# A graph network's gated step: one PSUM bank per graph in the last layer's gates

## The chip, the core and the metric

The kernel runs on one core of a Trainium2 chip. The core has a matrix engine (TensorE, PE in the profile), VectorE (DVE), ScalarE (ACT), GpSimd (POOL) and a queue engine for transfers (SyncE, SP). Matrix products are written to PSUM, eight banks of 512 f32 values for each of 128 partitions; PE writes them, ScalarE and VectorE read them. The metric is the time of one execution on the device, in microseconds (us); the median of three runs is given.

## The reference, cut to what matters

128 graphs of 128 nodes with 256 features each, and a 0/1 adjacency matrix per graph. First a normalisation and three layers of a gated network, then an attention layer. One gated layer is:

```
m    = h @ weight[i]
aggr = einsum('bst,bsd->btd', A, m)
gi   = aggr @ w_ih.T + b_ih          # split into i_r, i_z, i_n
gh   = h @ w_hh.T + b_hh             # split into h_r, h_z, h_n
r    = sigmoid(i_r + h_r)
z    = sigmoid(i_z + h_z)
n    = tanh(i_n + r * h_n)
h    = (1 - z) * n + z * h
```

Per graph the r and z gates thus need one sum over two products (state and edges), while n needs the two products apart: four blocks of columns, h_n, r, z, i_n.

## The kernel before, in words

The graphs are taken in 32 groups of 4. A group goes through three layers, called steps or turns here; the steps of three groups are interleaved by the list `turns`, so there are 96 gated steps in all. Steps of layers 0 and 1 (`gru`) compute the gates with features on partitions; the last layer's step (`gru_rows`) computes them with nodes on partitions, so that its result lies as the attention needs it.

The 2 x 2 blocks of each weight product are done in seven products in place of eight, with sums of blocks prepared ahead (`block_sums` for weights, `node_sums` for data). `products` writes the seven in order and adds them up in three pairs of PSUM banks, x, y and q. Each pair is one bank "rz" and one bank "n", each a tile of its own: x_rz, x_n, y_rz, y_n, q_rz, q_n. Two more banks, misc, serve the rest. The order is: product 1 into x, copied to y; product 5 (7 in the last step) into q; product 6 into y, copied to t2 in SBUF; the next into y, copied to t3, to which q is added by VectorE; then product 2 into x, one more into y, one more into q, which is added to t2. After that x, y, t2 and t3 each hold the sums for one quarter of the outputs; ScalarE takes the tanh of r and z from them, VectorE combines them with n.

In steps of layers 0 and 1 the data moves and the weights stand in the array: bank rz holds r and z for two graphs (256 columns each), bank n the two parts of n. In the last step the data stands in the array and the weights move: bank rz holds, for each of two graphs, r and z (a product of 256 columns), bank n for each graph h_n and i_n (products of 128 columns). There x and q are filled beforehand with the biases ("seeds", `seed`, from seed_x and seed_q). An f32 product stands as two records in the profile.

All work is recorded as operations with an engine, an assumed duration and the buffers (or parts of them) that they read and write. `Plan.run` orders them with these assumed durations, by due times; products of the gates keep their order as a chain. Then the operations are issued in that order, each engine working through its own list. Semaphores are not written by hand: the framework below derives them from the order and from which tiles each instruction reads and writes. Tiles are made by `make` from the table `BUFS`.

Names and lines of the profile: products of layers 0 and 1 are line 694, of the last step line 701; copies out of PSUM `put`, line 733 (737 and 739 for n with a bias); VectorE's addition of q, line 743; seeds, line 726; tanh of the gates, lines 789 and 807 (last step 837); edge sums, line 621; attention's products, lines 650 and 1077.

Of the kernel before, what the change touches and what calls it, by code (L numbers as in the profile page):

```python
# [16 lines left out]
P = 128  # L17
# [198 lines left out]
def kernel(  # L216
# [67 lines left out]
        "w1_sum": (1, "all", const, [P, D]),  # L284
    }
    DTYPE = {"at": I32, "a": BF16, "pl": U16, "plT": U16, "pe": U16, "peT": U16, "p3": BF16}
    phys = {}

    def make(tag, n, kind, pool, shape):
        for s in range(SETS if kind == "set" else 1):  # L290
            for k in range(n):
                phys[tag, s, k] = pool.tile(shape, DTYPE.get(tag, F32), name=f"{tag}_{s}{k}")
# [47 lines left out]
    def nat(b):  # L340
        return plain(b)[:, :3 * KD * D].rearrange("p (c e) -> p c e", e=D)

    def turned(src, dst, evict):

        for a in range(2):
            for k in range(KD):
                ps = bank()

                def turn(k=k, a=a, ps=ps):
                    for c in range(3):  # L350
                        nc.tensor.transpose(flat(ps)[:, c * P:(c + 1) * P],
                                            nat(src)[:, 3 * a + c, k * P:(k + 1) * P], ident)
                op("PE", 330, turn, [(src, a, a + 1)], [ps])
                to_sbuf(evict[k % len(evict)], 3 * P, ps, dst[k], 3 * P * a)

# [24 lines left out]
    def weights():  # L380
# [47 lines left out]
        homes = [[buf("h1"), last("hT")] for _ in range(L)]  # L428
        for layer in range(L):
            if layer == 1:  # L430
                turned(w_hh_nat, w_hhT, ("DVE", "ACT"))
                block_sums(w_hhT, W["s_hh"], "POOL", 1000)
            wT, half, msg = uT[layer // 2], layer % 2, w_msg[layer]
            for e in range(KD):
                ps = bank(layer == 0)

                def turn(ps=ps, e=e, msg=msg):
                    for k in range(KD):
                        nc.tensor.transpose(flat(ps)[:, k * P:(k + 1) * P],
                                            square(msg)[:, k, e * P:(e + 1) * P], ident)  # L440
                op("PE", 220, turn, [msg], [ps])
                to_sbuf("ACT", D, ps, wT, half * GN + e * D)
            w_x = homes[layer]
            for k in range(KD):
                for g0, gn in ((0, 512), (512, 3 * D - 512)):
                    ps = bank(layer == 0)

                    def compose(k=k, g0=g0, gn=gn, ps=ps, wT=wT, half=half):
                        for e in range(KD):
                            nc.tensor.matmul(  # L450
                                flat(ps)[:, :gn],
                                ap(wT)[:, half, e * D + k * P:e * D + (k + 1) * P],
                                plain(w_ihT[e])[:, g0:g0 + gn], start=(e == 0), stop=(e == KD - 1))
                    op("PE", 4 * gn * 27 // 32, compose,
                       [(wT, half * GN, (half + 1) * GN)] + w_ihT, [ps])
                    to_sbuf("DVE", gn, ps, w_x[k], g0)
            block_sums(w_x, W[f"s_x{layer}"], *(("POOL", 1000) if layer else ("DVE", 560)))
            if layer == 0:
                load_msg(2, [W["s_x0"]])
# [13 lines left out]

        def seeds():
            nc.gpsimd.tensor_tensor(plain(tmp[0]), plain(tmp[0]), plain(tmp[1]), OP.add)
            for t, q in ((tmp[0], 0), (tmp[2], 2)):
                nc.gpsimd.tensor_copy(ap(W["seed_x"])[:, q:q + 2, :], halves(t, 0))
                nc.gpsimd.tensor_tensor(ap(W["seed_q"])[:, q:q + 2, :], halves(t, 1), halves(t, 0),
                                        OP.subtract)
        op("POOL", 4000, seeds, tmp, [W["seed_x"], W["seed_q"]] + tmp[:1])  # L480

# [190 lines left out]
    DATA = [None, 0, 2, 3, 7, 4, 6, 5]  # L672
    R, Z, NN = 0, 1, 2

    def product(bank, i, parts, first, rows=False):


        def unit(t, w):
            return (t, DATA[i], DATA[i] + 1) if DATA[i] < 4 else (w, DATA[i] - 4, DATA[i] - 3)

        def source(t, w):
            if DATA[i] < 4:
                return ap(t)[:, DATA[i] // 2, (DATA[i] % 2) * H:(DATA[i] % 2 + 1) * H]
            return ap(w)[:, DATA[i] - 4, :]

        todo = []
        for term in range(max(len(p) for _, p in parts)):
# [3 lines left out]
        for c, chunk in enumerate(todo):  # L691
            def mm(c=c, chunk=chunk):
                for m, (half, q, w, t, sums) in enumerate(chunk):
                    nc.tensor.matmul(ap(bank)[:, half, :], ap(w)[:, i - 1, q, :], source(t, sums),  # L694
                                     start=(first and c == 0 and m == 0), stop=False,
                                     skip_group_check=True)

            def mm_rows(chunk=chunk):
                half, q, w, t, sums = chunk[0]
                for m in range(2):  # L700
                    nc.tensor.matmul(  # L701
                        ap(bank)[:, m, half * P:(half + len(chunk)) * P],
                        source(t, sums)[:, m * N:(m + 1) * N],
                        ap(w)[:, i - 1, q:q + len(chunk), :].rearrange("p q m -> p (q m)"),
                        start=False, stop=False, skip_group_check=True)
            plan.cursor += 432 * len(chunk) * SLOT // GATES
            op("PE", 432 * len(chunk), mm_rows if rows else mm,
               [unit(t, s) for _, _, _, t, s in chunk] + [(w, i - 1, i) for _, _, w, _, _ in chunk],
               [bank], due=plan.cursor)

    def products(layer, hT, hs, aT, gs, rows=False):

# [6 lines left out]
        state, edges = (W["s_hh"], hT, hs), (W[f"s_x{layer}"], aT, gs)  # L719
        kinds = (("rz", ((R, (state, edges)), (Z, (state, edges)))),  # L720
                 ("n", ((NN, (state,)), (NN, (edges,)))))
        X, Y, Q, T2, T3 = ({} for _ in range(5))

        def seed(b, kind, t):
            q = 0 if kind == "rz" else 2
            op("ACT", 590, lambda: nc.scalar.copy(
                ap(b), ap(t)[:, q:q + 2].rearrange("p (o q) m -> p o (q m)", o=1)
                .to_broadcast([P, 2, 2 * P])), [t], [b])

        def put(t, y, bias=None, mark=None):  # L730

# [13 lines left out]
        for kind, parts in kinds:  # L745
            X[kind], Y[kind] = buf("x_" + kind), buf("y_" + kind)
            if rows:
                seed(X[kind], kind, W["seed_x"])
            product(X[kind], 1, parts, not rows, rows=rows)
            put(Y[kind], X[kind], 1 if kind == "n" else None, mark=(plan.group, layer, kind))  # L750
        for kind, parts in kinds:
            Q[kind] = buf("q_" + kind)
            if rows:
                seed(Q[kind], kind, W["seed_q"])
            product(Q[kind], five, parts, not rows, rows=rows)
        for kind, parts in kinds:
            product(Y[kind], 6, parts, False, rows=rows)
            T2[kind] = buf("t2_" + kind)
            put(T2[kind], Y[kind], 2 if kind == "n" else None)
        for kind, parts in kinds:  # L760
            product(Y[kind], seven, parts, False, rows=rows)
            T3[kind] = buf("t3_" + kind)
            put(T3[kind], Y[kind])
            add(T3[kind], Q[kind])
        for kind, parts in kinds:
            product(X[kind], 2, parts, False, rows=rows)
        for kind, parts in kinds:
            product(Y[kind], four, parts, False, rows=rows)
        for kind, parts in kinds:
            product(Q[kind], three, parts, False, rows=rows)  # L770
            add(T2[kind], Q[kind])

        y, t2 = ((0, 1), (1, 0)) if rows else ((1, 0), (0, 1))
# [52 lines left out]
    def gru_rows(layer, hT, hs, aT, gs, rows, x1):  # L826
# [6 lines left out]
        for j, n, src in blocks:  # L833
            i = 2 * n + j
            outs, graphs = slice(j * P, (j + 1) * P), slice(2 * n, 2 * n + 2)
            s_rz, nn = src["rz"], src["n"]
            op("ACT", 700, lambda outs=outs, graphs=graphs, s_rz=s_rz: nc.scalar.activation(
                ap(rz).rearrange("p q (g d) -> p g q d", g=G)[:, graphs, :, outs],
                ap(s_rz).rearrange("p g (q m) -> p g q m", q=2), AF.Tanh, scale=0.5),
               [s_rz], [(rz, i, i + 1), (rz, 4 + i, 5 + i)])  # L840
            op("DVE", 422, lambda outs=outs, graphs=graphs, nn=nn: nc.vector.scalar_tensor_tensor(
                view(u)[:, graphs, outs],
                ap(rz)[:, 0].rearrange("p (g d) -> p g d", g=G)[:, graphs, outs], 1.0,
                ap(nn)[:, :, 0:P], op0=OP.add, op1=OP.mult),
               [nn, (rz, i, i + 1)], [(u, i, i + 1)], two=nn.tag[0] == "t")
            op("DVE", 422, lambda outs=outs, graphs=graphs, nn=nn: nc.vector.scalar_tensor_tensor(
                view(u)[:, graphs, outs], view(u)[:, graphs, outs], 0.5, ap(nn)[:, :, P:2 * P],
                op0=OP.mult, op1=OP.add),
               [nn], [(u, i, i + 1)], two=nn.tag[0] == "t")
        for n in (1, 0):  # L850
            d, lo, hi = buf("d"), 2 * n, 2 * n + 2
            cols = slice(n * GN, (n + 1) * GN)
# [340 lines left out]
```

## Time and profile before

| what | us |
|---|---|
| median of three runs | 2104.47 (2102.91 to 2105.32) |
| the profiled execution's own time | 2102.59 |
| its span, first to last instruction | 2100.6 |
| TensorE busy | 2086.8 (99%) |
| TensorE weight loads | 1862.0 (89%) |
| VectorE busy | 1668.5 (79%) |
| ScalarE busy | 1592.4 (76%) |
| GpSimd busy | 938.0 (45%) |

Records of matrix products overlap: a record lasts longer than the distance to the next one's start, so what a product costs is read from start to start in the timeline. A line of the timeline gives start, duration, engine, line, operation, tiles (out<-in), shape and number of merged records; in brackets stands the engine's idle time before it and who ended it. A line of the waits gives who waited for whom, the total in us, the number of times and the longest.

### The profile page before, as it was taken

Reading aid. Unit: us, or ns where it says so; the run is one execution under the profiler, and the core shown is the slowest. Engines: PE = TensorE matmul, PEld = TensorE weight load, DVE = VectorE, ACT = ScalarE, POOL = GpSimd, SP = SyncE. Lnnn points to the kernel's source line nnn. Section 1 sums busy time; section 2 is a strip of 40 time slices with the busy share of each in tenths; the row PEclk is TensorE's granted clock in tenths of the full one; section 3 lists DMA queues with packets and bytes.
Section 4 is the critical chain, followed back from the end, with each engine's and each line's share of the span. In section 5 each row is a group of like instructions: output and inputs, shape, how many; then the busy total and the mean of one; then the engine's idle time right before and its main releaser. Section 6 shows DMA issues by size and latency. Waiting matters only on the chain.

```text
span 2100.6 us, 33940 instructions
## 1 busy us (share of the span) xinstructions
PE 2086.8 (99%) x12416; PEld 1862.0 (89%) x12416; DVE 1668.5 (79%) x3370; ACT 1592.4 (76%) x2849; POOL 938.0 (45%) x881
## 2 busy tenths in 40 slices
PE   9999999999999999999999999999999999999998
PEld 6888888898888998898988889988989888988887
DVE  7777888888877888877888778888778887778778
ACT  6577878777878777777778787777777787777676
POOL 5545454345443445544454434455444544335330
PEclk9999999999999999999999999999999999999999
DMA  4323223232233222233222332222322223222331
GB/s 131 61 51 56 53 49 81 61 59 63 69 74 76 57 60 64 68 81 66 52 65 68 73 76 56 61 64 69 80 66 57 60 64 78 56 51 51 76 76 36
DMA packets 365158, 137.21 MB, mean 65 GB/s; under 512 B 296384, under 2 KB 364736, under 8 KB 364992
## 3 DMA queue, kind: packets, MB, share of 16 engines
q1 hardware_dynamic: 364992, 135.05, 28.5%
q8 instruction: 97, 1.59, 0.3%
q14 instruction: 69, 0.57, 0.1%
HBM read 45.36 MB, written 16.78 MB: 30 GB/s over the span
## 4 chain that ended last, share of the span: by engine, by line
PE 97%; DVE 2%; ACT 1%; issue 0%; DMA 0%; DVEq 0%
PE y_rz L694 16%; PE q_rz L694 11%; PE x_rz L694 10%; PE y_n L694 8%; PE y_rz L701 8%; PE misc L621 6%; PE x_n L694 5%; PE q_n L694 5%; PE q_rz L701 5%; PE x_rz L701 5%; PE misc L1077 5%; PE y_n L701 4%; PE x_n L701 3%; PE q_n L701 3%; PE misc L650 2%; PE misc L450 0%
## 5 line engine op out<-in xcount | busy, mean ns | idle before, releaser
L578 POOL TENSOR_TENSOR r<-rows 128x512 f32<-128x512 f32 x126 | 136.1, 1100 | 268.0 <-ACT rows L561 183.4
L733 ACT COPY t_rz<-y_rz 128x512 f32<-128x512 f32 x192 | 112.4, 585 | 178.8 <-PE y_rz L694 89.5
L743 DVE TENSOR_TENSOR t_rz<-t_rz,q_rz 128x512 f32<-128x512 f32 x192 | 131.2, 684 | 98.0 <-ACT t_rz L733 57.0
L603 POOL TENSOR_TENSOR pl<-d,pl 128x512 bf16<-128x512 f32 x64 | 74.7, 1170 | 294.1 <-ACT pl L601 293.9
L694 PE MATMUL y_rz<-hs,s_hh 128*128 128x256 f32 x768 | 197.5, 380 | 0.0
L694 PE MATMUL y_rz<-gs,s_x 128*128 128x256 f32 x768 | 197.1, 379 | 0.0
L668 POOL TENSOR_TENSOR hs<-hT,hs 128x256 f32<-128x256 f32 x96 | 81.8, 852 | 241.6 <-PE q_n L701 173.7
L664 POOL TENSOR_TENSOR hs<-hT 128x512 f32<-128x512 f32 x96 | 130.4, 1358 | 100.4 <-ACT hT L561 32.1
L694 PEld LDWEIGHTS y_rz<-gs,s_x 128*128 128x128 f32 x768 | 145.9, 190 | 19.8
L694 PEld LDWEIGHTS y_rz<-hs,s_hh 128*128 128x128 f32 x768 | 143.1, 190 | 18.8 <-issue 0.5
L581 POOL TENSOR_TENSOR p<-r 128x512 bf16<-128x512 f32 x126 | 153.2, 1235 | 0.0
L743 DVE TENSOR_TENSOR t_n<-t_n,q_n 128x512 f32<-128x512 f32 x192 | 131.2, 683 | 20.5 <-ACT t_n L733 8.2
L694 PE MATMUL x_rz<-hT,s_hh 128*128 128x256 f32 x512 | 131.5, 379 | 0.0
L694 PE MATMUL x_rz<-aT,s_x 128*128 128x256 f32 x512 | 131.4, 379 | 0.0
L624 ACT COPY aT<-misc 128x512 f32<-128x512 f32 x190 | 110.5, 584 | 13.6 <-PE misc L621 9.6
L501 DVE BATCH_NORM_STATS2 st<-rows 128x6 f32<-128x256 f32 x128 | 45.1, 413 | 94.6 <-DMA rows<-in_x_dram 94.5
L816 DVE TENSOR_TENSOR d<-hT,u 128x512 f32<-128x512 f32 x128 | 110.6, 864 | 8.9 <-ACT u L813 8.7
L694 PE MATMUL y_n<-hs,s_hh 128*128 128x256 f32 x384 | 114.4, 379 | 0.0
L694 PE MATMUL y_n<-gs,s_x 128*128 128x256 f32 x384 | 114.2, 379 | 0.0
L598 POOL TENSOR_TENSOR d<-hT,pl 128x512 f32<-128x512 f32 x64 | 90.8, 1421 | 51.4 <-ACT pl L596 45.6
L1077 PE MATMUL misc<-w,uT 128*128 128x256 f32 x480 | 113.3, 380 | 0.3 <-ACT uT L655 0.3
L694 PEld LDWEIGHTS x_rz<-aT,s_x 128*128 128x128 f32 x512 | 97.2, 190 | 13.2
(277 smaller groups left out, 6500.6 us busy)
## 6 DMA issues: line engine op xcount, KB each, us to landing
rows<-in_x_dram SPq DMA_DIRECT2D x32, 512.0 KB, 4.2
x<-in_x_dram SPq DMA_DIRECT2D x32, 512.0 KB, 3.9
out_dram<-x SPq DMA_DIRECT2D x31, 512.0 KB, 2.9
at<-in_adj_dram SPq DMA_DIRECT2D x32, 256.0 KB, 2.8
plT<-pl SPq DMA_TRANSPOSE x186, 3.3
peT<-pe SPq DMA_TRANSPOSE x60, 3.1
e<-in_L_gnn_weight_dram SPq DMA_DIRECT2D x3, 256.0 KB, 3.2
rz<-in_L_gnn_w_ih_dram SPq DMA_DIRECT2D x2, 384.0 KB, 3.9
```

The lines of the kernel that those rows point to most:

```text
L578: op("POOL", 1106, lambda part=part: nc.gpsimd.tensor_tensor(ap(r1)[:, part], ap(rows)[:, part], top(rows)[:, part], OP.subtract), [(rows, ...
L581: op("POOL", 1050, lambda part=part: nc.gpsimd.tensor_tensor(ap(p3)[:, part], ap(r1)[:, part], top(r1)[:, part], OP.subtract), [(r1, n, n ...
L598: op("POOL", 1150, lambda k=k, r=r: nc.gpsimd.tensor_tensor(ap(r), ap(hT)[:, k], part(pl, k, 0), OP.subtract), [(hT, 2 * k, 2 * k + 2), (p ...
L621: nc.tensor.matmul(flat(ps)[:, b * N:(b + 1) * N], part(i, b, k), ap(a)[:, b, :], start=(i == 0), stop=(i == 2))
L624: op("ACT", 590, lambda k=k, ps=ps: nc.scalar.copy(ap(dst)[:, k, :], flat(ps)), [ps], [(dst, 2 * k, 2 * k + 2)])
L664: op(eng, cost, lambda: sub(ap(w)[:, 0:2, :], blocks()[:, 1::2, :], blocks()[:, 0:2, :], OP.subtract), [t], [(w, 0, 2)], two=True)
L694: nc.tensor.matmul(ap(bank)[:, half, :], ap(w)[:, i - 1, q, :], source(t, sums), start=(first and c == 0 and m == 0), stop=False, skip_gro ...
L701: nc.tensor.matmul(ap(bank)[:, m, half * P:(half + len(chunk)) * P], source(t, sums)[:, m * N:(m + 1) * N], ap(w)[:, i - 1, q:q + len(chun ...
L733: op("ACT", 590, lambda: nc.scalar.copy(ap(t), ap(y)), [y], [t], mark=mark)
L743: op("DVE", 690, lambda: nc.vector.tensor_tensor(ap(t), ap(t), ap(q), OP.add), [q], [t])
L816: op("DVE", 690, lambda j=j, d=d, cols=cols: nc.vector.tensor_tensor(ap(d), ap(hT)[:, j, :], ap(u)[:, cols], OP.subtract), [(hT, lo, hi), ...
L1077: nc.tensor.matmul(ap(ps)[:, b, :], ap(uT)[:, k, (m + b) * N:(m + b + 1) * N], ap(w1)[:, k, :], start=(k == 0), stop=(k == KD - 1))
```

## The change

In `make`, the tiles whose names end in _rz and _n (x, y, q in PSUM, t2 and t3 in SBUF) become one tile of two banks' size each; the former names are its two halves. In the last step a half now belongs to one of the two graphs and holds h_n, r, z and i_n side by side. A product of the state covers the first 384 columns (h_n, r, z), a product of the edges the last 384 (r, z, i_n), so one product takes the place of one of 256 and one of 128 columns. The state's weights are turned with the n gate first, the seeds stand in the new order, and the readers of the last step take both halves at once. Layers 0 and 1 keep their products; they use the joined tiles and pick the state's gates in the new order.

```diff
-    phys = {}
+    phys, both = {}, {}
 
     def make(tag, n, kind, pool, shape):
+        name, _, half = tag.partition("_")
+        if shape == [P, 2, H] and half:
+            if half == "rz":
+                both[name] = pool.tile([P, 2, 2, H], F32, name=name)
+            phys[tag, 0, 0] = both[name][:, ("rz", "n").index(half)]
+            return
...
-                turned(w_hh_nat, w_hhT, ("DVE", "ACT"))
+                turned(w_hh_nat, w_hhT, ("DVE", "ACT"), (4, 5, 0, 1, 2, 3))
...
-            for t, q in ((tmp[0], 0), (tmp[2], 2)):
+            for t, q in ((tmp[0], slice(1, 3)), (tmp[2], slice(0, 4, 3))):
...
-            def mm_rows(chunk=chunk):
-                half, q, w, t, sums = chunk[0]
-                for m in range(2):
-                    nc.tensor.matmul(
-                        ap(bank)[:, m, half * P:(half + len(chunk)) * P],
-                        source(t, sums)[:, m * N:(m + 1) * N],
-                        ap(w)[:, i - 1, q:q + len(chunk), :].rearrange("p q m -> p (q m)"),
-                        start=False, stop=False, skip_group_check=True)
...
+                    gate = (q + 1) % 3 if w is W["s_hh"] else q
...
+    def product_rows(bank, i, m, sources):
+        for c, (w, t, sums) in enumerate(sources):
+            plan.cursor += 645 * SLOT // GATES
+            op("PE", 645, lambda c=c, w=w, t=t, sums=sums: nc.tensor.matmul(
+                flat(bank)[:, c * P:(c + 3) * P], source(i, t, sums)[:, m * N:(m + 1) * N],
+                ap(w)[:, i - 1].rearrange("p q m -> p (q m)"), start=False, stop=False,
+                skip_group_check=True), [unit(i, t, sums), (w, i - 1, i)], [bank], due=plan.cursor)
...
+        if rows:
+            kinds = (("rz", 0), ("n", 1))
...
-            op("ACT", 590, lambda: nc.scalar.copy(
-                ap(b), ap(t)[:, q:q + 2].rearrange("p (o q) m -> p o (q m)", o=1)
-                .to_broadcast([P, 2, 2 * P])), [t], [b])
+            op("ACT", 590, lambda: nc.scalar.copy(flat(b), plain(t)), [t], [b])
...
-                ap(s_rz).rearrange("p g (q m) -> p g q m", q=2), AF.Tanh, scale=0.5),
-               [s_rz], [(rz, i, i + 1), (rz, 4 + i, 5 + i)])
+                ap(rz).rearrange("p q (g d) -> p g q d", g=G)[:, graphs, :, outs], sums[:, :, 1:3, :],
+                AF.Tanh, scale=0.5), banks_of, [(rz, i, i + 1), (rz, 4 + i, 5 + i)])
```

More of the change, by code (lines that the diff above doesn't have):

```diff
@@ L341, in nat, with turned @@
         return plain(b)[:, :3 * KD * D].rearrange("p (c e) -> p c e", e=D)
-    def turned(src, dst, evict):
+    def turned(src, dst, evict, order=range(6)):
         for a in range(2):
@@ L351, in turn @@
                         nc.tensor.transpose(flat(ps)[:, c * P:(c + 1) * P],
-                                            nat(src)[:, 3 * a + c, k * P:(k + 1) * P], ident)
+                                            nat(src)[:, order[3 * a + c], k * P:(k + 1) * P],
+                                            ident)
                 op("PE", 330, turn, [(src, a, a + 1)], [ps])
@@ L475, in seeds @@
             nc.gpsimd.tensor_tensor(plain(tmp[0]), plain(tmp[0]), plain(tmp[1]), OP.add)
-            for t, q in ((tmp[0], 0), (tmp[2], 2)):
-                nc.gpsimd.tensor_copy(ap(W["seed_x"])[:, q:q + 2, :], halves(t, 0))
-                nc.gpsimd.tensor_tensor(ap(W["seed_q"])[:, q:q + 2, :], halves(t, 1), halves(t, 0),
+            for t, q in ((tmp[0], slice(1, 3)), (tmp[2], slice(0, 4, 3))):
+                nc.gpsimd.tensor_copy(ap(W["seed_x"])[:, q, :], halves(t, 0))
+                nc.gpsimd.tensor_tensor(ap(W["seed_q"])[:, q, :], halves(t, 1), halves(t, 0),
                                         OP.subtract)
@@ L673, with unit, source, product @@
     R, Z, NN = 0, 1, 2
[L675 to L684, printed above, removed]
+    def unit(i, t, w):
+        return (t, DATA[i], DATA[i] + 1) if DATA[i] < 4 else (w, DATA[i] - 4, DATA[i] - 3)
+    def source(i, t, w):
+        if DATA[i] < 4:
+            return ap(t)[:, DATA[i] // 2, (DATA[i] % 2) * H:(DATA[i] % 2 + 1) * H]
+        return ap(w)[:, DATA[i] - 4, :]
+    def product(bank, i, parts, first):
         todo = []
@@ L693, in mm @@
                 for m, (half, q, w, t, sums) in enumerate(chunk):
-                    nc.tensor.matmul(ap(bank)[:, half, :], ap(w)[:, i - 1, q, :], source(t, sums),
+                    gate = (q + 1) % 3 if w is W["s_hh"] else q
+                    nc.tensor.matmul(ap(bank)[:, half, :], ap(w)[:, i - 1, gate, :], source(i, t, sums),
                                      start=(first and c == 0 and m == 0), stop=False,
                                      skip_group_check=True)
-            def mm_rows(chunk=chunk):
-                half, q, w, t, sums = chunk[0]
-                for m in range(2):
-                    nc.tensor.matmul(
-                        ap(bank)[:, m, half * P:(half + len(chunk)) * P],
-                        source(t, sums)[:, m * N:(m + 1) * N],
-                        ap(w)[:, i - 1, q:q + len(chunk), :].rearrange("p q m -> p (q m)"),
-                        start=False, stop=False, skip_group_check=True)
             plan.cursor += 432 * len(chunk) * SLOT // GATES
-            op("PE", 432 * len(chunk), mm_rows if rows else mm,
-               [unit(t, s) for _, _, _, t, s in chunk] + [(w, i - 1, i) for _, _, w, _, _ in chunk],
+            op("PE", 432 * len(chunk), mm,
+               [unit(i, t, s) for _, _, _, t, s in chunk] + [(w, i - 1, i) for _, _, w, _, _ in chunk],
                [bank], due=plan.cursor)
+    def product_rows(bank, i, m, sources):
[5 more added lines that the diff above has]
+                skip_group_check=True), [unit(i, t, sums), (w, i - 1, i)], [bank], due=plan.cursor)
     def products(layer, hT, hs, aT, gs, rows=False):
@@ L721, in products, with add_product, seed @@
                  ("n", ((NN, (state,)), (NN, (edges,)))))
-        X, Y, Q, T2, T3 = ({} for _ in range(5))
-        def seed(b, kind, t):
-            q = 0 if kind == "rz" else 2
-            op("ACT", 590, lambda: nc.scalar.copy(
-                ap(b), ap(t)[:, q:q + 2].rearrange("p (o q) m -> p o (q m)", o=1)
-                .to_broadcast([P, 2, 2 * P])), [t], [b])
+        if rows:
+            kinds = (("rz", 0), ("n", 1))
+        def add_product(bank, i, parts, first):
+            if rows:
+                product_rows(bank, i, parts, (state, edges))
+            else:
+                product(bank, i, parts, first)
+        X, Y, Q, T2, T3 = ({} for _ in range(5))
+        def seed(b, t):
+            op("ACT", 590, lambda: nc.scalar.copy(flat(b), plain(t)), [t], [b])
         def put(t, y, bias=None, mark=None):
@@ L747, in products @@
             if rows:
-                seed(X[kind], kind, W["seed_x"])
-            product(X[kind], 1, parts, not rows, rows=rows)
+                seed(X[kind], W["seed_x"])
+            add_product(X[kind], 1, parts, not rows)
             put(Y[kind], X[kind], 1 if kind == "n" else None, mark=(plan.group, layer, kind))
@@ L753, in products @@
             if rows:
-                seed(Q[kind], kind, W["seed_q"])
-            product(Q[kind], five, parts, not rows, rows=rows)
+                seed(Q[kind], W["seed_q"])
+            add_product(Q[kind], five, parts, not rows)
         for kind, parts in kinds:
-            product(Y[kind], 6, parts, False, rows=rows)
+            add_product(Y[kind], 6, parts, False)
             T2[kind] = buf("t2_" + kind)
@@ L760, in products @@
         for kind, parts in kinds:
-            product(Y[kind], seven, parts, False, rows=rows)
+            add_product(Y[kind], seven, parts, False)
             T3[kind] = buf("t3_" + kind)
@@ L765, in products @@
         for kind, parts in kinds:
-            product(X[kind], 2, parts, False, rows=rows)
+            add_product(X[kind], 2, parts, False)
         for kind, parts in kinds:
-            product(Y[kind], four, parts, False, rows=rows)
+            add_product(Y[kind], four, parts, False)
         for kind, parts in kinds:
-            product(Q[kind], three, parts, False, rows=rows)
+            add_product(Q[kind], three, parts, False)
             add(T2[kind], Q[kind])
@@ L835, in gru_rows @@
             outs, graphs = slice(j * P, (j + 1) * P), slice(2 * n, 2 * n + 2)
-            s_rz, nn = src["rz"], src["n"]
-            op("ACT", 700, lambda outs=outs, graphs=graphs, s_rz=s_rz: nc.scalar.activation(
-                ap(rz).rearrange("p q (g d) -> p g q d", g=G)[:, graphs, :, outs],
-                ap(s_rz).rearrange("p g (q m) -> p g q m", q=2), AF.Tanh, scale=0.5),
-               [s_rz], [(rz, i, i + 1), (rz, 4 + i, 5 + i)])
-            op("DVE", 422, lambda outs=outs, graphs=graphs, nn=nn: nc.vector.scalar_tensor_tensor(
+            banks_of = [src["rz"], src["n"]]
+            sums = both[src["rz"].tag.split("_")[0]].rearrange("p g a m -> p g (a m)").rearrange(
+                "p g (q m) -> p g q m", q=4)
+            sbuf = src["rz"].tag[0] == "t"
+            op("ACT", 700, lambda outs=outs, graphs=graphs, sums=sums: nc.scalar.activation(
+                ap(rz).rearrange("p q (g d) -> p g q d", g=G)[:, graphs, :, outs], sums[:, :, 1:3, :],
+                AF.Tanh, scale=0.5), banks_of, [(rz, i, i + 1), (rz, 4 + i, 5 + i)])
+            op("DVE", 422, lambda outs=outs, graphs=graphs, sums=sums: nc.vector.scalar_tensor_tensor(
                 view(u)[:, graphs, outs],
                 ap(rz)[:, 0].rearrange("p (g d) -> p g d", g=G)[:, graphs, outs], 1.0,
[L844 to L849, printed above, removed]
+                sums[:, :, 0, :], op0=OP.add, op1=OP.mult),
+               banks_of + [(rz, i, i + 1)], [(u, i, i + 1)], two=sbuf)
+            op("DVE", 422, lambda outs=outs, graphs=graphs, sums=sums: nc.vector.scalar_tensor_tensor(
+                view(u)[:, graphs, outs], view(u)[:, graphs, outs], 0.5, sums[:, :, 3, :],
+                op0=OP.mult, op1=OP.add), banks_of, [(u, i, i + 1)], two=sbuf)
         for n in (1, 0):
```

## The prediction

> **What bounds the kernel now.** I read the page's shares and its chain first, then stretches of time, then the timeline of one step, then the waits.
>
> ```profile
> PE 2086.8 (99%) x12416; PEld 1862.0 (89%) x12416; DVE 1668.5 (79%) x3370; ACT 1592.4 (76%) x2849; POOL 938.0 (45%) x881
> ...
> PE 97%; DVE 2%; ACT 1%; issue 0%; DMA 0%; DVEq 0%
> ```
>
> TensorE holds 97% of the chain that ended last. By stretches:
>
> ```profile
> 560.00:1060.00 500.00, 500.00 (x2992) 448.84 (x2992) 398.58 (x817) 387.13 (x686) 225.94 (x210) 1.00 0.30 66
> ```
>
> In 500 us of the middle PE has no gap at all, at the full clock. So time here is the sum of PE's start-to-start times plus PE's waits, and a PE wait that appears anywhere is paid in full. The timeline of one last step, PE's rows and one of ScalarE's:
>
> ```profile
> 1026.50 1.03 PE L701 MATMUL y_rz<-s_hh,hs 128*128 128x256 f32 x4
> ...
> 1027.37 1.03 PE L701 MATMUL y_rz<-s_x,gs 128*128 128x256 f32 x4
> ...
> 1028.23 0.61 PE L701 MATMUL y_n<-s_hh,hs 128*128 128x128 f32 x4
> ...
> 1028.48 0.59 ACT L733 COPY t_rz<-y_rz 128x512 f32<-128x512 f32 x1 [1.67 <-PE y_rz L701]
> ...
> 1028.67 0.61 PE L701 MATMUL y_n<-s_x,gs 128*128 128x128 f32 x4
> ...
> 1029.12 1.89 PE L1077 MATMUL misc<-w,uT 128*128 128x256 f32 x8
> ```
>
> Each f32 product is two records. Eight records of 256 columns take 1028.23 - 1026.50 = 1.73 us, 216 ns each; eight of 128 take 0.89 us, 111 ns each (median of all start-to-start times 112; records of 512 columns, line 450, 429). And note the copy: ScalarE reads y_rz from 1028.48 to 1029.07 while PE goes on writing y_n. That overlap is what the change touches. The waits say who is early there:
>
> ```profile
> ACT t_rz L733 <- PE y_rz L694: 89.5, 97, 3.6
> ACT t_rz L733 <- PE y_rz L701: 89.1, 58, 2.0
> ```
>
> In 155 of 192 such copies ScalarE stood idle until PE was done: the reader follows PE at once, PE never waits for it.
>
> **What the Trainium skill says.** "TensorE: Matmul & The Clock Gate", section "Back-to-back issue gap", gives N/2.4 + 2.5 ns. The bf16 products of the trace fit (128 columns: 55.8, measured 56). f32 records take twice the streaming part: 2 x 256/2.4 + 2.5 = 215.8 against 216, 512 columns 429.2 against 429; so a record of 384 is an estimate of 322.5 ns, and it lies on the line between the two measured widths. The same page, "LDWEIGHTS (loading the stationary operand)", says columns/1.2, 107 ns for 128; below it shows up after a wait. "PSUM — Partial Sum Buffer", section "PSUM bank collisions raise a hardware error", says that two engines on different banks run clean. So a wait between two banks comes from how the program tracks its tiles, not from the chip; no run here shows it otherwise. "Engine vs sequencer instructions" on that page says that matmuls start and complete in program order: what stands behind a waiting product waits too,; at 2043.54, shown further down, PE sat 1.47 us with all its other work behind one product.
>
> **Part 1, wider products.** For each of 7 products, 2 sources, 2 graphs, 2 records and 32 last steps = 1792 pairs, a record of 256 and one of 128 (216 + 112 = 328) become one of 384 (322.5). Saved: 1792 x 5.5 ns = 9.9 us; with 109 or 114 in place of 112 it is 4 to 13. The built program has 6494 products for 7390, 896 fewer; no other compute count changes on any engine.
>
> **Part 2, seeds and weights in another order.** The same number of copies and sums of the same sizes; the four order lists cost nothing, POOL (45%) and ScalarE hide them, and without cover they would cost the same as before.
>
> **Part 3, later reads in the last step.** Both banks must be done before a tanh (597 ns) can start, where r and z were done some 0.9 us before n. The bank is needed again two products, 5 us, later, so it hides; only at the kernel's end, where nothing follows, it shows: about 1 us, 0 to 2.
>
> **Part 4, the joined tiles.** `make` now gives x, y, q (and t2, t3) one tile of two banks each, for all 96 steps, not for the 32 last ones alone. In the built order PE's rows read so in a last step (names of semaphores in brackets):
>
> ```
> L717 Matmult y<-s_hh_157,hs_85 128x384
> L717 Matmult y<-s_x_00_160,gs_89 128x384
> L717 Matmult y<-s_hh_157,hs_85 128x384
> L717 Matmult y<-s_x_00_160,gs_89 128x384 [waits Activation_49]
> ```
>
> The third and fourth row write the second bank. The value that the fourth waits for is the copy t2<-y of the first bank; that copy in turn waits for a count that the third row posts. The whole tile is tracked, not its banks. Before, nothing stood between the two: this is the overlap at 1028.48 turned into a round trip PE, ScalarE, PE with no PE work under it. I followed every wait of PE back in this way, through the queue of the waiting-for engine, and summed the PE work that stands between. With less than 0.3 us under it: 3 waits before, 301 in the changed program, evenly over its length (23 to 39 per 200 us of PE work), 222 of them in the first two layers' steps (line 703), 72 in the last steps' products (line 717), 7 at start and end. By what PE waits for: copies t2<-y and t3<-y 119; y<-x 38; the gates' tanh out of PSUM 60; VectorE's t2 += q 58; the pair of n copies 15; 11 others, 3 of them old. In nearly all exactly one instruction lies between.
>
> The price of one round trip is shown once in the trace before, with no PE work under it:
>
> ```profile
> 16.84 0.60 PE L531 MATMUL misc<-ident,rows 128*128 128x128 f32 x4
> ...
> 17.47 0.59 ACT L534 COPY hT<-misc 128x512 f32<-128x512 f32 x1 [0.49 <-PE misc L531]
> ...
> 18.11 1.16 PE L636 MATMUL misc<-r,rows 128*128 128x128 f32 x8 [0.67 <-ACT hT L534]
> ```
>
> PE idles 0.67 us (0.03 to the copy's start, 0.59, 0.05 back). The drain that pipelining hides comes on top: a record lasts 275 where the next starts after 112 (379 and 216 for the wide one), 0.16. After the wait a weight load lies bare: 1.16 for eight records where line 650 has 1.05, 0.11. Sum 0.94, that is the instruction's duration plus 0.355. The second sample, the wait with a few other things ahead:
>
> ```profile
> 2043.54 1.13 PE L701 MATMUL y_rz<-s_hh,hs 128*128 128x256 f32 x4 [1.47 <-ACT t_rz L733]
> ```
>
> It has the same 0.10 (1.13 for 1.03). With durations from the rows of before:
> copies (586) 119 x 0.94 = 112; y<-x (570) 38 x 0.925 = 35; tanh (467, line 789) 60 x 0.82 = 49; adds (684, line 743) 58 x 1.04 = 60; pairs (471 + 368) 15 x 1.19 = 18; 8 others at 1.3 = 10. Sum 284 us.
>
> To this comes that the engine between may be late: in the trace before, copies of y_rz start 37 ns (median) and 0.25 us (mean) after PE. PE's pauses give ScalarE and VectorE 13% more time, so I take 0.08 x 298 = 24; bounds 0 and 75. Waits with 0.3 to 0.9 us of PE work under them are 54 for 20; at most a few hundred ns each is uncovered: 5, bounds 0 and 15. Queued behind each stalled product is all of PE's work; nobody else is hurt, since everybody else gains slack.
>
> **Sum against the profiled execution:** span 2100.6 - 9.9 + 1 + 284 + 24 + 5 = 2404.7; the three stalls of over 1 us that the middle and end have now (200, 2041, and their like) lose about 3 to the new pauses: 2402. The profiled run took 2102.6 with a span of 2100.6, the median of runs is 2104.5, 3.9 over the span: 2406 us, rounded to 2405.
>
> **The rivals.** (A) As summed, 2405, its own range 2345 to 2470. (B) The waits are there but satisfied when PE comes to them, and only part 1 counts: 2104.5 - 9.9 = 2094.6, faster. For it: the copies follow PE within 40 ns, and PE has weight loads it could do early. Against it: it decides only if over 0.94 us of PE work lies between release and wait, and the order shows none. (C) The pauses cascade: a copy that is late makes the next one late, since ScalarE waits for VectorE in 653 places for 565; at the mean lateness of 0.25 or twice that, 298 x 0.42 more, 2530. Against it: both engines have idle time in every slice and gain more. (D) Only the last steps pay, if the first two layers' waits had cover that I fail to see: 72 x 0.95 - 10 = 58, 2163.
>
> **How the numbers follow.** A 0.83, C 0.11, D 0.02, B 0.04. A measurement of this kernel can tell about 0.2% (4 us) from no change. Slower 0.96, faster 0.03, same 0.01. The range is A's own, whose ends are all prices at 0.8 (284 to 227) and the lateness at its upper bound with prices 5% up, 2345 to 2470; it leaves C's tail, B and D out.
>
> **What would show it.** PE's busy share falls from 99% to 87 to 90%. The waits list PE <- ACT on t2, t3, y<-x and the gates, and PE <- DVE on t2, some 300 times at about 0.67 to 0.8 each, led by line 703. Start-to-start of the 384 records is 322 ns. The chain gets ScalarE at 7% or more and VectorE at 3%. If PE's waits are few, part 4 is wrong; if they are 300 but twice as long, C.

## The result

The changed kernel takes 2399.9 us (2398.9 to 2400.6, 4 runs), the one before 2104.0 us, run beside it: ratio 1.1406, 95% interval 1.1386 to 1.1425. It is 296 us slower, with 896 products fewer. The profiled execution's span went from 2100.6 to 2398.8 us.

The page's shares of the changed kernel:

```profile
PE 2166.2 (90%) x10624; PEld 1641.8 (68%) x10624; DVE 1696.8 (71%) x3370; ACT 1609.0 (67%) x2849; POOL 924.1 (39%) x881
```

PE has 1792 records fewer, and still its share falls from 99% to 90%; ScalarE and VectorE have as many instructions as before, in a longer time. By stretches of time, after:

```profile
560.00:1060.00 500.00, 455.78 (x2256) 346.83 (x2257) 360.90 (x709) 342.88 (x601) 191.27 (x182) 1.00 0.26 57
```

The stretch that was full of PE work now has 44 us in 500 without any, at the same clock. The same place of a last step as was shown of before, from the timeline of after:

```profile
1182.32 0.81 PE L717 MATMUL y<-s_hh,hs 128*128 128x384 f32 x2
...
1183.16 0.59 ACT L749 COPY t<-y 128x512 f32<-128x512 f32 x1 [1.82 <-PE y L717]
...
1183.80 0.30 PEld L717 LDWEIGHTS y<-s_x,gs 128*128 128x128 f32 x2 [1.29 <-ACT t L749]
1183.80 0.91 PE L717 MATMUL y<-s_x,gs 128*128 128x384 f32 x2 [0.68 <-ACT t L749]
...
1184.55 0.81 PE L717 MATMUL x<-s_hh,hT 128*128 128x384 f32 x2
...
1185.19 0.81 PE L717 MATMUL x<-s_x,aT 128*128 128x384 f32 x2
```

The products (MATMUL) at 1182.32 and 1183.80 write the second bank of y, the copy reads the first. The copy starts when the product at 1182.32 has ended, though it reads nothing of it, and the next product of the second bank starts 0.05 us after the copy's end. Both directions of the false dependence stand here. From 1182.32 to 1183.80 there are 1.48 us where two records take 0.64 (1184.55 to 1185.19), and the two records after the wait take 0.75 (1183.80 to 1184.55): 0.94 us lost in all. The weight loads (PEld) of the waiting product start only with it, at 1183.80. The waits of PE after, those with most time first:

```profile
PE y L703 <- ACT t L749: 48.3, 69, 0.7
PE y L717 <- ACT t L749: 38.1, 55, 1.2
PE q L703 <- DVE t L759: 36.6, 47, 1.0
PE x L703 <- ACT y L749: 21.8, 32, 0.7
...
PE x L703 <- ACT rz L805: 13.6, 24, 0.6
```

Before, the longest entry of PE was this:

```profile
PE y_rz L701 <- ACT t_rz L733: 2.8, 2, 1.5
```

Line 703 holds the products of layers 0 and 1, which were not changed.

PE's time can be split by the starts of its records. The sum of the undisturbed start-to-start times (112, 216, 322.5 and 429 ns for f32 records of 128, 256, 384 and 512 columns, 56 for bf16 records of 128) went from 2073.0 to 2063.1, that is 9.9 less. What lies above that sum went from 22.3 to 329.7, that is 307.4 more.

### The profile page after: what moved, and what is told of

Its sections match the earlier page's. It is cut to its first block, busy times and chain, and to the rows that moved or that the text cites. A ratio compares the mean times of both kernels' runs of the same rounds, so it can differ in the third digit from the quotient of the medians.

```text
span 2398.8 us, 30229 instructions
## 1 busy us (share of the span) xinstructions
PE 2166.2 (90%) x10624; PEld 1641.8 (68%) x10624; DVE 1696.8 (71%) x3370; ACT 1609.0 (67%) x2849; POOL 924.1 (39%) x881
## 5 line engine op out<-in xcount | busy, mean ns | idle before, releaser
L759 DVE TENSOR_TENSOR t<-t,q 128x512 f32<-128x512 f32 x384 | 259.1, 686 | 271.3 <-ACT t L749 155.8
L703 PE MATMUL y<-gs,s_x 128*128 128x256 f32 x1152 | 323.6, 390 | 79.8 <-ACT t L749 48.3
L749 ACT COPY t<-y 128x512 f32<-128x512 f32 x320 | 184.1, 587 | 307.0 <-PE y L703 175.2
L703 PE MATMUL y<-hs,s_hh 128*128 128x256 f32 x1152 | 314.2, 382 | 5.4 <-ACT t L755 5.4
L703 PEld LDWEIGHTS y<-gs,s_x 128*128 128x128 f32 x1152 | 209.1, 189 | 150.8 <-ACT t L749 76.0
L703 PE MATMUL x<-aT,s_x 128*128 128x256 f32 x768 | 213.5, 387 | 35.9 <-ACT y L749 21.8
L703 PEld LDWEIGHTS y<-hs,s_hh 128*128 128x128 f32 x1152 | 216.0, 190 | 37.1 <-ACT t L755 7.9
L703 PE MATMUL x<-hT,s_hh 128*128 128x256 f32 x768 | 207.6, 379 | 0.0
L703 PEld LDWEIGHTS x<-aT,s_x 128*128 128x128 f32 x768 | 141.1, 190 | 75.4 <-ACT y L749 34.4
L703 PEld LDWEIGHTS x<-hT,s_hh 128*128 128x128 f32 x768 | 145.8, 190 | 26.0
```

Of the source, the lines that this page charges most:

```text
L703: nc.tensor.matmul(ap(bank)[:, half, :], ap(w)[:, i - 1, gate, :], source(i, t, sums), start=(first and c == 0 and m == 0), stop=False, sk ...
L749: op("ACT", 590, lambda: nc.scalar.copy(ap(t), ap(y)), [y], [t], mark=mark)
L759: op("DVE", 690, lambda: nc.vector.tensor_tensor(ap(t), ap(t), ap(q), OP.add), [q], [t])
```

## The experiments

**The joined tiles alone, and nothing else of the change.** The kernel before, with `make` putting the two banks of the named pairs in one tile:

```diff
-    phys = {}
+    phys, both, JOINED = {}, {}, ('x', 'y', 'q', 't2', 't3')
...
+        name, _, half = tag.partition("_")
+        if name in JOINED and half in ("rz", "n"):
+            if half == "rz":
+                both[name] = pool.tile([P, 2, 2, H], F32, name=name)
+            phys[tag, 0, 0] = both[name][:, ("rz", "n").index(half)]
+            return
```

> The kernel before with joined tiles alone (x, y, q, t2, t3), its products of 256 and 128 columns kept. Theory (the joined tile makes PE wait for the reader of the other bank): the built order has 390 new waits with less than 0.3 us of PE work under them (157 for copies into t2 and t3, of which 12 pairs; 82 for VectorE's t2 += q; 111 for tanh; 32 for y<-x). At the instruction's duration plus 0.355 us that is about 365, with lateness and half-covered waits about 380: 2484, range 2440 to 2530. It is slower than the changed kernel, since that one has 298 such waits. Rival (the last step's new layout, with readers that need both banks, makes the loss): 2104, within 10.

Measured 2512.6 us, ratio 1.1944 (1.1922 to 1.1965). The joining makes the whole loss, and more of it than the changed kernel has. From its waits of PE:

```profile
PE y L700 <- ACT t L739: 63.9, 90, 0.7
PE q L700 <- DVE t L749: 43.4, 56, 0.8
...
PE x L700 <- ACT rz L795: 36.4, 48, 1.0
```

The same pairs as in the changed kernel, more often. The rival, the last step's layout as the cause, is out: that layout isn't in this kernel. The time is 29 us over the forecast. Of PE's starts that come over 0.15 us late there are 448, where the kernel before has 21, so some 427 are new and not 390. More of the half-covered waits cost something than the forecast held: 63 starts are late for y<-x, where it counted 32 without cover.

**The tiles in SBUF alone.** The same edit with only t2 and t3 named.

> The kernel before with t2 and t3 joined, in SBUF, and x, y, q left as two tiles each. Theory (only the PSUM tiles cost): no new wait of PE in the built order, 2104 within 5. Rival (all joined tiles are waited for as a whole, so ScalarE and VectorE hold each other up at t2 and t3 and PE behind them): 2130 or more.

Measured 2103.55 us against 2103.72, ratio 0.9998 (0.9990 to 1.0007). Joining the halves of these SBUF tiles costs nothing here; the loss is made by the PSUM tiles of two banks. Whether the two halves of an SBUF tile are tracked apart, or together without anyone having to wait longer, this run does not show.

**One PSUM pair alone, and the price of a wait.** The same edit with only q named.

> The kernel before with q alone joined. Theory: 86 new waits, 82 of them for VectorE's t2 += q at 684 + 355 ns, 3 for seeds, sum about 89, with lateness 3: 2196, range 2180 to 2215. Rival (a wait costs what PE sits idle, about 0.75 us, and drain and weight load are hidden): 2168. Rival (pauses overlap with other waits): below 2160.

Measured 2200.3 us, ratio 1.0459 (1.0445 to 1.0474): 96.6 us, where 92 were forecast for 86 waits. Its waits of PE:

```profile
PE q L700 <- DVE t_rz L749: 46.3, 55, 3.0
PE q L707 <- DVE t_rz L749: 22.0, 28, 0.9
```

83 waits show 68.3 us of idle PE, 0.82 us each. The late starts show the rest: a start after such a wait is 0.98 us late on average (median 0.94), and the record after it 0.106 us more. So a wait costs 1.05 to 1.08 us, not the 0.75 or 0.82 that the column of idle time shows. 83 x 1.084 = 90. Of the remaining 7 us, four waits for the seed copies of q make 3.5, and a stretch at half clock, described with the run of x alone, makes 1.4.

**The same waits, with a shorter instruction waited for.** In the kernel with q joined, VectorE adds only the first half of the columns of each bank of q to t2; the second half of that sum is left out, the order and the waits are the same.

```diff
-            op("DVE", 690, lambda: nc.vector.tensor_tensor(ap(t), ap(t), ap(q), OP.add), [q], [t])
+            part = slice(0, 1) if t.tag[:2] == "t2" else slice(0, 2)
+            op("DVE", 690, lambda: nc.vector.tensor_tensor(
+                ap(t)[:, part], ap(t)[:, part], ap(q)[:, part], OP.add), [q], [t])
```

> The kernel with q alone joined, and VectorE's t2 += q done on the first half of its columns only (the second half of that sum is left out); the order and all waits stay as with q joined. Theory (a new wait costs the duration of the instruction waited for plus a fixed 0.355 us): each of 82 waits is shorter by some 0.26 us (684 against about 420 ns), 22 us in all: 2178.5, within 5. Rival (the cost is a fixed one of the round trip, whatever the duration): 2200.

Measured 2172.4 us, ratio to the kernel before 1.0329 (1.0312 to 1.0347), 27.8 us less than with the whole addition (2200.3). The waits of PE, and the group of the shortened additions (line, engine, operation, tiles and shapes, count, busy us, mean ns, idle before):

```profile
PE q L700 <- DVE t_rz L750: 30.7, 55, 2.4
PE q L707 <- DVE t_rz L750: 14.6, 28, 0.6
```

```profile
L750 DVE TENSOR_TENSOR t_rz<-t_rz,q 128x256 f32<-128x256 f32 x96 | 40.2, 418 | 71.4 <-PE q L700 41.9 <-PE q L707 29.3
```

As many waits, 83, and 45.3 us for 68.3: 0.277 us less for each, where the addition is 684 - 418 = 0.266 shorter. The duration of the instruction waited for is in the price one to one. 23 us of the 27.8 are these. Of the other 5, two waits for copies of y (late by 0.9 us in place of 1.6 each) make 1.4 us, and the stretch at half clock, which this run does not have, another 1.4; the rest was not taken apart.

**x alone, and y alone.** The same edit with one name.

> The kernel before with x alone joined. Built order: 83 new waits without cover (50 for tanh of x, 32 for y<-x, one at the end), 71 us at duration plus 0.355; 32 more with 0.3 to 0.9 us of PE work under them, which the run with all tiles joined showed at about 0.5 us each: 16. 2192, range 2170 to 2210. Rival (the costs of the three tiles are shared, the largest hides the others): below 2150.

Measured 2236.0 us, ratio 1.0627 (1.0606 to 1.0648): 132 us, not 88. The number of waits is as forecast, the price isn't:

```profile
PE x L700 <- ACT rz L795: 65.4, 48, 2.2
PE x L700 <- ACT y_rz L739: 19.0, 28, 0.8
```

48 waits for the tanh of x stand at 1.36 us of idle PE each, and 22 of PE's starts are over 2 us late. One of these in the timeline:

```profile
1146.88 0.59 PE L700 MATMUL x<-hT,s_hh 128*128 128x256 f32 x2
...
1148.03 0.68 DVE L749 TENSOR_TENSOR t_rz<-t_rz,q_rz 128x512 f32<-128x512 f32 x1
...
1148.74 0.51 ACT L795 ACTIVATE rz<-t_rz,bias_s 128x256 f32<-128x256 f32 x1 [1.11 <-DVE t_rz L749]
1149.16 0.46 ACT L795 ACTIVATE rz<-x,bias_s 128x256 f32<-128x256 f32 x1
...
1149.66 0.70 PE L700 MATMUL x<-aT,s_x 128*128 128x256 f32 x2 [2.19 <-ACT rz L795]
```

The tanh that PE waits for stands in ScalarE's queue behind another tanh, and that one waits 1.11 us for VectorE, which is busy until 1148.71 with an addition on t. The forecast had counted the one instruction between, as if its engine were free. In the kernel before, ScalarE is as late at these 22 places: the tanh starts 1.70 us (median) after the end of the product before, for 1.70 here, and nobody waits for it. Such a start costs 2.47 us with the record after it, where the forecast had 0.82: 22 x 1.65 = 36 of the 44 us.

Most of the rest is a slower clock. In six stretches of 3.41 us the granted clock was 0.5, and the products of 256 columns then took 427 ns from start to start in place of 216; that is 9.5 us in all. Each stretch begins 0.6 to 1.4 us after one of the 22 long waits; the changed kernel has two such stretches (3.3 us), the one with q joined has one, each at the end of a PE pause of 1.8 us or more or within 1.5 us after it, and the kernel before has none in the middle. Not every long pause is followed by one (16 of the 22 are not), and why was not tested.

> The kernel before with y alone joined. Built order: 221 new waits without cover (145 for copies into t2 and t3, 12 for pairs, 63 for tanh of y), 205 us at duration plus 0.355; half covered ones and lateness 19: 2328, range 2305 to 2350. If waits add up one by one, x, y and q alone together lose what the run with all joined lost, 409 us, within 15; if they overlap, more than that.

Measured 2319.4 us, ratio 1.1023 (1.1001 to 1.1045): 215 us for 224 forecast. The three alone lose 132 + 215 + 97 = 444 us, the three together 409 (2512.6 - 2103.7). So they overlap, beyond the 15 us allowed for. Most of it stands at one place. The order of instructions on each engine is the same in these runs, and the same 48 waits for the tanh of x take 65.4 us of PE with x alone and 36.4 with all joined; at the 22 places the tanh now starts 0.50 us after the product's end, not 1.70. So the pauses of PE for y and q give ScalarE and VectorE time to catch up. The half clock of the run with x alone, 9.5 us, is the other part: with all joined there is none.

**The wide products without the joined PSUM tiles.** The changed kernel with x_rz, x_n and the like as tiles of their own again. The last step's readers of x and y then take one bank each: two instructions where there was one.

```diff
-        if shape == [P, 2, H] and half:
+        if name in ("t2", "t3"):
...
-            op("ACT", 700, lambda outs=outs, graphs=graphs, sums=sums: nc.scalar.activation(
-                ap(rz).rearrange("p q (g d) -> p g q d", g=G)[:, graphs, :, outs], sums[:, :, 1:3, :],
-                AF.Tanh, scale=0.5), banks_of, [(rz, i, i + 1), (rz, 4 + i, 5 + i)])
...
+                parts = [(slice(2 * n + k, 2 * n + k + 1), lambda b=b: ap(b).rearrange(
+                    "p (o a) m -> p o (a m)", o=1).rearrange("p o (q m) -> p o q m", q=4), [b]) for k, b in enumerate(banks_of)]
+            scale = len(parts)
+            for graphs, sums, reads in parts:
+                op("ACT", 700 // scale + 100 * (scale - 1), lambda outs=outs, graphs=graphs, sums=sums: nc.scalar.activation(
+                    ap(rz).rearrange("p q (g d) -> p g q d", g=G)[:, graphs, :, outs], sums()[:, :, 1:3, :],
+                    AF.Tanh, scale=0.5), reads, [(rz, i, i + 1), (rz, 4 + i, 5 + i)])
```

(VectorE's two products with n are split in the same way; readers of t2 and t3 stay whole.)

> The changed kernel with x, y, q as two tiles each again; t2 and t3 stay joined. Products of 384 columns stay. The readers of x and y in the last step are two instructions, one per bank (tanh and both products with n), 2 tanh and 4 VectorE instructions more in each of 32 steps. Theory: no new wait of PE in the built order, and 9.9 us less of products: 2094 to 2097, faster than before. Rival (the wide products or the later reads are themselves a loss): 2104 or more. Rival (the added readers make ScalarE and VectorE late): 2100 to 2115.

Measured 2094.5 us (2093.6 to 2094.7, 5 runs), ratio 0.9955 (0.9941 to 0.9969): faster than both. The page's shares, and the same stretch of time:

```profile
PE 2078.5 (99%) x10624; PEld 1663.2 (79%) x10624; DVE 1701.6 (81%) x3498; ACT 1609.5 (77%) x2913; POOL 950.5 (45%) x881
```

```profile
560.00:1060.00 500.00, 500.00 (x2558) 401.63 (x2557) 409.28 (x849) 397.22 (x709) 232.17 (x210) 1.00 0.30 67
```

PE is full again. Its undisturbed sum is the 2063.1 us of the changed kernel; what lies above it is 24.5 us against 22.3 before. So the wide products bring their 9.9 us; 2.2 of these go again, at both ends of the run: the first 60 us have 2.8 and the last 90 us 2.4 us more above the sum, the middle 3.1 less. Of the 2.8, 1.6 are one wait for a transfer of weights that stands ahead of every gated step. The 64 tanh and 128 VectorE instructions that were added are hidden.

## Why the prediction was right

It said 2405 (2345 to 2470) and slower; 2399.9 was measured.

**What bounds the kernel.** Right, and it carried the rest: with no gap in PE's middle, each new wait was paid in full.

**Part 1, wider products.** Right to the digit that can be read: the median start-to-start of the 1792 records of 384 columns is 323 ns (322.5 was estimated from the formula in the Trainium skill, "TensorE: Matmul & The Clock Gate", section "Back-to-back issue gap", with its streaming part doubled, and from the widths on both sides), the sum is 9.9 us less. The run without joined PSUM tiles shows it as 9.2 us of time, with the losses at the ends in it.

**Parts 2 and 3.** Hidden as said, but for the ends. The run with separate tiles has 2.4 us more above the sum in its last 90 us, part 3's "1 us, 0 to 2" being somewhat too small; which of the later reads or the other order does it was not separated.

**Part 4, count.** Right. Late starts of PE by over 0.15 us, by what they waited for, measured against forecast: t copies 124 for 119, y<-x 40 for 38, tanh 60 for 60, VectorE's addition 64 for 58, pairs of n copies 24 for 15. The 22 beyond the count are probably waits that the forecast had put among the half-covered; they were not followed one by one.

**Part 4, price.** Right, because it was summed from a stall of the same kind with its drain and its bare weight load. Measured, as the late start plus the record after it: t copies 860 + 104 = 964 ns for 940; y<-x 936 for 925; tanh 835 for 820; additions 994 for 1040, with a median of 1047; pairs 973 for 1190, some of them half covered. The five kinds sum to 124 x 0.964 + 40 x 0.936 + 60 x 0.835 + 64 x 0.994 + 24 x 0.973 = 294 us of the 307.4. Of the other 13, three waits for the seed copies of q make about 7 and the two stretches at half clock about 3; the half clock is a cost that the forecast did not have.

**The two small terms.** Lateness was set at 24 us and is smaller: the idle time per t copy is 0.70 us, where 0.67 is the round trip itself, so 0.03 us in place of 0.08, some 9 us in all. The half-covered waits, set at 5 us, seem larger instead: the 22 late starts beyond the count, at 0.95 us, are about 21. The two errors, some 15 us each, nearly cancel, and that is luck.

**The rivals.** (B), waits satisfied in time, is out: 312 of PE's starts show them. (D), only the last steps pay, is out: line 703 has the larger part of the waits. (C), pauses that cascade, is not in this kernel, whose waits stand near their bare price; only the three waits for seeds are longer. But the run with x alone joined shows that waits behind a queue exist: 22 of them, with 2.2 us of idle PE each. With y and q joined too, in the same order, the same 22 starts are 1.17 us late and not 2.37. That supports the prediction's argument (everybody gains slack), but the slack comes from the other pauses: with those for x alone it did not reach. How much this kernel's other order helped was not tested.

**What could not be read.** The chain that ended last is followed in the profile after for only 16% of the span, so the forecast that ScalarE would hold 7% of it can't be judged.

## What to carry to other kernels

The view over two PSUM banks was had by making them one tile, and one tile of two banks was tracked here as one thing: writes to one bank waited for the readers of the other, in all 96 steps and not only in the 32 that wanted the view. Before joining buffers, look in the built order for producer-side waits on readers of the other half with no work between; their number times (duration + 0.36 us) estimates the loss, as long as the engine that is waited for is free when its turn comes. Where it is not, the loss is larger: 132 us for 88 with x alone. Where the readers can be split per bank instead, the gain of the wider product comes without these waits: here it cost small extra instructions on engines that had idle time, and spared waits on the one that had none.

## What the runs showed of the hardware

A round trip of PE to another engine and back costs more than PE's idle time says. For a copy of 587 ns the idle column shows 0.70 us, and PE loses 0.96: about 0.16 is the drain that the next product would have covered (a record of 384 columns lasts 486 ns where the next starts after 323), 0.10 the weight load that stands bare afterwards. The record after a wait starts 0.10 us late in every kernel here (101 to 104 ns as the mean of nearly every kind of wait); the two weight loads of the product at 1183.80 start 109 ns apart. That is close to the 107 ns that the formula in the Trainium skill, "TensorE: Matmul & The Clock Gate", section "LDWEIGHTS (loading the stationary operand)", comes to for 128 columns. An f32 record of 384 columns takes 323 ns start to start, on the line between 216 for 256 and 429 for 512 columns; one of 128 takes 112, 2 to 3 ns above that line.
